# A graph kernel: the permuted graph written over the graph itself, and new shares of the pipeline

## The chip, the cores and the metric

The kernel runs on one core of one Trainium2 chip. The metric is the device time in microseconds of one execution. Engines are named as in the profile: PE (TensorE, matmuls), PEld (its weight loads), DVE (VectorE), ACT (ScalarE), POOL (GpSimd) and SP (SyncE, which issues the transfers).

## The reference

Thirty-two graphs of 512 nodes with 64 features each pass through four layers; after each layer comes x = layernorm(x + layer(x)). Layer 0 averages over neighbours, layer 1 is a Chebyshev filter of order 4, layer 2 a hyperbolic attention over all pairs of nodes, and layer 3 takes quantiles over each node's neighbours. The edited code prepares layer 3:

```python
nb = (adj_ > 0) & (~eye)[None]
m = nb.sum(-1)
rank = jnp.cumsum(nb, axis=-1) - 1
skip = jnp.where(m > T_THRESH, (m + K_DIL - 1) // K_DIL, 1)
removed = nb & do_dil[..., None] & ((rank + 1) % skip[..., None] == 0)
rem = removed | jnp.swapaxes(removed, 1, 2)
adj_d = jnp.where(rem, 0.0, adj_)
# then, for each node and feature: sort the features of its neighbours in adj_d,
# and add up the interpolated quantiles 0.25, 0.5, 0.75 with weights 0.25, 0.5, 0.25
```

## The kernel before

The kernel does not loop over graphs at run time. It records every operation of all 32 graphs (`Order.op`), and a planner (`Order.issue`) then fixes one program order for each engine. An operation belongs to a lane of a graph: front (layers 0 and 1), pairs and tail (layer 2), graph (the code above), gather (fetches the neighbours' features by matmul with one-hot matrices), sort (a sorting network on DVE for nodes in two strips, SB), and head (the strip of the nodes with most neighbours, SH, for two graphs at a time, and the final dense layers). "ends" and "check" run once, near the end.

`STAGES` (line 1415) gives each lane a pair of numbers: the part of the pipeline period, counted from the graph's own number, at which the lane's first and last operations are due. The planner always issues the ready operation with the earliest due time; on PE it stays with the present shape of matmul (64 or 128 columns of weights, 64 or 128 rows) unless another is due much earlier. Where PE would be idle in its plan, it puts in filler matmuls (`stay_active`, lines 1451 to 1454), after leaving a first part of the gap open:

```python
for _ in range(int((t - spare - fill) / 0.11)):   # line 387, fill = 0.3
```

Buffers matter too. A tile is asked for with a tag, and tiles of one tag share a number of buffers. A new tile of a tag is given out only when the last reader of the old one is over. The graph lane has three big tiles of one buffer each, with tags nbT, v and V, each 128 x 4 x 512 in 16-bit floats.

The steps of the graph lane for one graph: nbT marks the neighbours (lines 789 to 791). Matmuls of nbT with a triangular matrix count them in order, ACT and DVE turn the counts into the marks v of the edges to remove (809 to 815). Matmuls of v, its transpose and nbT give the thinned graph V, evicted by ACT with row sums (816 to 827). In `order`, the row sums give each node's position rk by size (834 to 846), and perm is the permutation matrix, made by DVE from it (850 to 852). Matmuls of V with perm give the permuted graph VP, evicted by ACT (853 to 858). Matmuls of VP with the triangular matrix number the neighbours of each node: slot (859 to 864). Matmuls with ones give the counts, from which ACT makes the small one-hot tiles OHM (865 to 875). The gather lane reads slot.

Before the change, perm has nbT's tag and VP has v's. The lane has one PSUM bank, so its matmul groups and their evictions alternate. ACT's program order also holds loads of activation tables, at every change between the logarithm and exponential functions and the sigmoid and tanh functions (lines 391 and 483).

Of the kernel before, what the change touches and what calls it, by code (L numbers as in the profile page):

```python
# [9 lines left out]
F16 = mybir.dt.float16  # L10
# [4 lines left out]
AF = mybir.ActivationFunctionType  # L15
# [5 lines left out]
P = 128  # L21
# [382 lines left out]
def tile_adj_resnorm(ctx: ExitStack, tc: tile.TileContext, x, adj, nodemask, w1k, b1k, att_w, att_b,  # L404
                     w1, b1, w2, b2, out):
    nc = tc.nc
    B, N, D = x.shape
    T = N // P
# [16 lines left out]
    seq = Order(nc, tc)  # L425

    def width(a):
        n = 1
        for d in a.ap[1:]:
            n *= d[1]  # L430
        return n
# [18 lines left out]
    def ts(out, a, s1, s2, op0, op1=None):  # L450
        kw = {} if op1 is None else {"op1": op1}
        vec(lambda: nc.vector.tensor_scalar(out, a, s1, s2, op0=op0, **kw), out, [a], True, (s1, s2))  # L452

    def stt(out, a, s, b, op0, op1):
        vec(lambda: nc.vector.scalar_tensor_tensor(out, a, s, b, op0=op0, op1=op1), out, [a, b], False, (s,))  # L455

    def cp(out, a):
        vec(lambda: nc.vector.tensor_copy(out, a), out, [a], True)
# [18 lines left out]
    def act(out, a, f, bias=None, scale=1.0, accum_out=None, after=None):  # L477
        sc = [x for x in (bias, scale) if isinstance(x, bass.AP)]
        kw = {k: v for k, v in (("bias", bias), ("accum_out", accum_out)) if v is not None}
        n = width(out)  # L480
        table = "exp" if f in (AF.Ln, AF.Exp) else "sig" if f in (AF.Sigmoid, AF.Tanh) else None
        seq.op("ACT", 0.12 + n * 0.83e-3 + 0.09 * len(sc) + (0.2 if accum_out is not None else 0.0),
             0.3, lambda: nc.scalar.activation(out, a, f, scale=scale, **kw), [out, accum_out], [a, after] + sc, table)  # L483
# [7 lines left out]
    def mm(out, w, a, start, stop, pair=False, opens=None):  # L491

        n, m = width(a), width(w)
        if a.dtype == F32:

            t = (1 if pair else 2) * max(0.9e-3 * m, 0.88e-3 * n)
        else:
            t = max(0.058, n * (0.24e-3 if m == D else 0.44e-3))
        def go():
            if opens is not None:  # L500
                seq.open = opens
            return nc.tensor.matmul(out, w, a, start=start, stop=stop)  # L502

        seq.op("PE", t, 0.6, go, [out], [w, a], (64 if w.ap[0][1] <= 64 else 128, 64 if m <= 64 else 128))

    def tr(out, a, ident):
        seq.op("PE", 0.115 if a.dtype == F32 else 0.058, 0.6, lambda: nc.tensor.transpose(out, a, ident), [out], [a, ident],
               (128, 64 if width(a) <= 64 else 128))
# [6 lines left out]
    def bank(dtype=F32, home=None):  # L515
        lane, seq.lane = seq.lane, home or seq.lane
        t = seq.tile(pools["ps"], [P, 512 if dtype == F32 else 1024], dtype, "bank", bufs=BANKS.get(seq.lane, 2))
        seq.lane = lane
        return t
# [21 lines left out]
    UC = const.tile([P, N], F16, name="UC")  # L541
# [3 lines left out]
    onesP = const.tile([P, P], F16, name="onesP")  # L545
# [161 lines left out]
    def col(name):  # L707
        return seq.tile(pools["small"], [P, T], F32, name, 2)
# [121 lines left out]
    def order(b, res):  # L830

        gm = pools["gm"]
        V = res["V"]
        key = col("key")
        stt(key, M3[:, b, :], float(N), iotr, op0=OP.mult, op1=OP.add)
        pt = bank()
        for t in range(T):
            tr(pt[:, t * P:(t + 1) * P], key[:, t:t + 1].to_broadcast([P, P]), identf)
        keyh = col("keyh")
        ts(keyh, key, -0.5, None, op0=OP.add)  # L840
        sg = col("sg")
        for t in range(T):
            junk = seq.tile(gm, [P, N], F16, "junk", 1)
            act(junk, pt, AF.Sign, bias=keyh[:, t:t + 1], scale=-1.0, accum_out=sg[:, t:t + 1])
        rk = col("rk")
        ts(rk, sg, -0.5, 0.5 * N - 1.0, op0=OP.mult, op1=OP.add)

        rkh = seq.tile(pools["keep"], [P, T], F16, "rkh", 8)
        cp(rkh, rk)
        perm = seq.tile(gm, [P, T, N], F16, "perm", 1, "nbT")  # L850
        for t in range(T):
            ts(perm[:, t, :], iotap, rk[:, t:t + 1], None, op0=OP.is_equal)
        VP = seq.tile(gm, [P, T, N], F16, "VP", 1, "v")
        for j in range(T):
            pt = bank()
            for t in range(T):
                mm(pt, V[:, t, j * P:(j + 1) * P], perm[:, t, :], start=(t == 0), stop=(t == T - 1))
            act(VP[:, j, :], pt, AF.Copy)
        slot = seq.tile(pools["keep"], [P, T, N], F16, "slot", 2)
        for j in range(T):  # L860
            pt = bank()
            for k in range(j + 1):
                mm(pt, UC[:, :P] if k == j else UC[:, P:2 * P], VP[:, k, :], start=(k == 0), stop=(k == j))
            act(slot[:, j, :], pt, AF.Copy)
        pt = bank()
        for k in range(T):
            mm(pt, onesP, VP[:, k, :], start=(k == 0), stop=(k == T - 1))
        if b % 2 == 0:
            res["ohm"] = OHM[:, b // 2 % 3]
        dist = seq.tile(gm, [P, H2], F16, "dist")  # L870
        for i in range(P // HM):
            hm, h = slice(i * HM, (i + 1) * HM), i % 2
            act(dist[hm], pt[hm, h * H2:(h + 1) * H2], AF.Abs, bias=npart[hm])
        for i, hm in enumerate((PADS, RANKS)):
            act(res["ohm"][hm, i, b % 2, :], dist[hm], AF.Relu, bias=1.0, scale=-1.0)
        res["slots"] = slot, rkh

    def stage_graph(b, res):
        graph(nmask[:, :, b], res["AT"], M3[:, b, :], res)
        order(b, res)  # L880
# [503 lines left out]
    def within_bounds():  # L1384

        gm, BT = pools["gm"], B * T
        seq.lane = "graph"
        p1, p2, p3 = bank(), bank(), bank()
        ge = [seq.tile(gm, [P, T, N], F16, "ge", 1, t).rearrange("p t n -> p (t n)") for t in ("nbT", "v")]
        ge = [ge[s % 2][:, s // 2 * BT:(s // 2 + 1) * BT] for s in range(K + 1)]  # L1390
        seq.lane = "check"
        m = M3.rearrange("p b t -> p (b t)")

        for s in range(K + 1):
            ts(ge[s], m, float(s), None, op0=OP.is_gt)
        for s in range(K + 1):
            mm(p1[:BT, s:s + 1], ge[s], onesP[:, 0:1], start=True, stop=True)
        cs = seq.tile(gm, [BT, K + 1], F16, "cs")
        act(cs, p1[:BT, :K + 1], AF.Copy)
        mm(p2[:B, :K + 1], graphs[:BT, :], cs, start=True, stop=True)  # L1400
        off = seq.tile(gm, [B, 2, K + 1], F16, "off")
        for i, op in enumerate((OP.is_gt, OP.is_lt)):
            tt(off[:, i, :], p2[:B, :K + 1], limits[:, i, :], op=op)
        bad = seq.tile(gm, [B, 1], F32, "bad")
        reduce(bad, off.rearrange("p i s -> p (i s)"), OP.max)
        badh = seq.tile(gm, [B, 1], F16, "badh")
        cp(badh, bad)
        mm(p3[:1, 0:1], badh, onesP[:B, 0:1], start=True, stop=True)
        ts(flag, p3[:1, 0:1], 0.0, None, op0=OP.is_gt)
# [2 lines left out]

    STAGES = {"front": (-0.6, -0.5), "pairs": (1.2, 1.3), "tail": (0.2, 1.5), "graph": (0.9, 1.0), "gather": (2.7, 2.9),
              "sort": (4.5, 4.6), "head": (4.7, 5.6), "ends": (4.0, 4.5), "check": (3.4, 4.8)}

    nc.scalar.preload_act_table_set("natural_log_exp_and_others")
    with ExitStack() as fast:
# [57 lines left out]
        within_bounds()  # L1477
        seq.issue(80.0, STAGES, stay_active, 0.3)
        seq.lane = "dense"
# [141 lines left out]
    with tc.If(flagv > 0):  # L1621
        with ExitStack() as slow:
# [24 lines left out]
            for h in range(4):  # L1647
                t = cst.tile([P, T, QC * ROWS], BF16, name=f"parts{h}")
# [32 lines left out]
def build(inputs):  # L1681
    import numpy as np
    import concourse.bacc as bacc

    nc = bacc.Bacc("TRN2", target_bir_lowering=False, num_devices=1)
    arrays, args = {}, []
    for name in _INS:
        a = np.ascontiguousarray(inputs[name])
        if a.dtype == np.bool_:
            a = a.view(np.uint8)  # L1690
        arrays[f"in_{name}_dram"] = a
        args.append(nc.dram_tensor(f"in_{name}_dram", a.shape, mybir.dt.from_np(a.dtype), kind="ExternalInput").ap())
    args.append(nc.dram_tensor("out_0_dram", inputs["x"].shape, F32, kind="ExternalOutput").ap())
    with tile.TileContext(nc) as tc:
        tile_adj_resnorm(tc, *args)
    return nc, arrays
# [8 lines left out]
```

## Time and profile before

| | us |
|---|---|
| median of three runs | 2626.49 |
| the three runs | 2620.58, 2626.49, 2630.43 |
| the profiled execution | 2622.02 |
| its span, first to last instruction | 2620.2 |

The span is what the profile divides among the engines; 1.8 us of the profiled execution lie outside it. The shares of busy time, the stretches and the waits that matter are shown in the prediction. Of the groups, these belong to the code that is edited:

```profile
L502 PE MATMUL graph_bank<-graph_perm,graph_V 128*128 128x512 f16 x512 | 141.0, 382 | 16.1 <-DVE graph_perm L452 13.8
L483 ACT ACTIVATE graph_VP<-graph_bank 128x512 f16<-128x512 f32 x128 | 75.5, 590 | 53.7 <-PE graph_bank L502 49.4
```

Each row gives the line, the engine, the tiles (out, then in), the shape and the number of instructions; then the busy time in us and the mean duration of one in ns; then the idle time of the engine just before them and what ended most of it. Nearly all operations are recorded by helpers, so a line is that of a helper (502 is `mm`, 483 is `act`, 448 is `tt`, 452 is `ts`, 455 is `stt`), and the tile's name, which begins with its lane, tells what the row is.

### The profile page before, as it was taken

To read this page: it belongs to the slowest core of one execution; us is meant where nothing else is said; L and a number is where in the kernel's file an instruction comes from. 1 tells how busy PE (TensorE), PEld (TensorE's weight loads), DVE (VectorE), ACT (ScalarE), POOL (GpSimd) and SP (SyncE) were. 2 spreads that over 40 slices of the span, in tenths; PEclk is the share of its full clock that TensorE was granted. 3 is DMA by queue.
4 is the path that set the end of the run, shared out by engine and by line. 5 is a ranking of instruction groups with operands and counts; after the bars stand their busy time and mean duration, and the time that the engine had idled before them with its cause. 6 is when DMAs were issued, how large, how long until landed. Compare 5 with 4: busy or idle time off the path is not lost.

```text
span 2620.2 us, 55667 instructions
## 1 busy us (share of the span) xinstructions
PE 2458.2 (94%) x19641; PEld 1635.4 (62%) x19667; DVE 2402.7 (92%) x9002; ACT 1879.2 (72%) x4406; POOL 815.8 (31%) x1783
## 2 busy tenths in 40 slices
PE   7999999999999999999999999999999999999997
PEld 6666566666666666666656666566666666666655
DVE  3668998999999999999999999999999999998996
ACT  5666677767777777767777677777777778776761
POOL 1233332332343333322333233333323333332210
PEclk9999999999999999999999899999999999998999
DMA  1100000000000000000000000000000000000000
GB/s 38 33 23 21 17 14 15 25 22 23 18 11 22 20 25 21 24 17 13 20 21 25 19 19 13 20 23 22 26 19 13 18 19 26 19 11 3 5 7 8
DMA packets 119723, 49.96 MB, mean 19 GB/s; under 512 B 53740, under 2 KB 119436, under 8 KB 119436
## 3 DMA queue, kind: packets, MB, share of 16 engines
q1 hardware_dynamic: 118272, 46.15, 6.4%
q8 instruction: 156, 2.56, 0.4%
q14 instruction: 131, 1.07, 0.1%
q10 hardware_dynamic: 1164, 0.18, 0.0%
HBM read 37.93 MB, written 8.39 MB: 18 GB/s over the span
## 4 chain that ended last, share of the span: by engine, by line
DVE 72%; PE 18%; ACT 6%; issue 2%; POOL 2%; DMA 0%; ACTq 0%; DVEq 0%
DVE SB L448 17%; DVE SH L448 8%; DVE gather_oh L452 6%; PE front_bank L502 5%; DVE pairs_Q L448 4%; PE gather_bank L502 3%; PE graph_bank L502 3%; DVE pairs_RW L448 3%; PE pairs_bank L502 3%; DVE sort_prod L448 3%; DVE pairs_Wt L455 3%; DVE pairs_L L455 2%; DVE tail_v L448 2%; DVE pairs_EX L448 2%; DVE pairs_RW L455 2%
## 5 line engine op out<-in xcount | busy, mean ns | idle before, releaser
L448 DVE TENSOR_TENSOR SB<-SB 128x448 f32<-128x448 f32 (+11 forms) x1424 | 565.8, 424 | 12.2 <-ACT SB L483 0.7
L502 PE MATMUL gather_bank<-gather_oh,tail_x3h 128*64 128x448 f16 (+5 forms) x5376 | 516.5, 321 | 4.8 <-ACT SB L483 3.4
L502 PEld LDWEIGHTS <-tail_x3h 128*64 128x64 bf16 x5376 | 296.0, 111 | 214.3 <-issue 112.8
L448 DVE TENSOR_TENSOR SH<-SH 128x32 f32<-128x32 f32 (+11 forms) x1744 | 347.4, 246 | 8.1
L502 PE MATMUL pairs_bank<-pairs_FT 67*128 67x512 f32 (+7 forms) x768 | 316.9, 516 | 18.7 <-ACT pairs_EX L483 7.1
L452 DVE TENSOR_SCALAR gather_oh<-graph_slot 128x256 f16<-128x256 f16 (+9 forms) x864 | 252.3, 337 | 25.3 <-PE gather_bank L502 23.5
L502 PE MATMUL front_bank<-front_AT,front_y 128*64 128x512 f32 x768 | 189.5, 607 | 18.5 <-DVE front_y L448 17.0
L502 PEld LDWEIGHTS pairs_bank<-pairs_FT 67*128 67x128 f32 (+1 forms) x768 | 130.2, 194 | 83.2 <-issue 19.7
L502 PE MATMUL graph_bank<-graph_perm,graph_V 128*128 128x512 f16 x512 | 141.0, 382 | 16.1 <-DVE graph_perm L452 13.8
L502 PEld LDWEIGHTS <-graph_nbT 128*128 128x128 f16 x1536 | 113.1, 99 | 57.6 <-issue 17.3
L722 POOL TENSOR_TENSOR front_rs<-front_var,mhalf 128x4 f32<-128x4 f32 x64 | 83.4, 1303 | 201.8 <-DVE front_var L452 152.9
L502 PEld LDWEIGHTS front_bank<-XA,front_AT 128*128 128x128 f32 x1024 | 126.0, 194 | 13.6 <-issue 6.3
L1453 PE MATMUL PA<-zero 128*128 128x256 bf16 x973 | 132.9, 278 | 0.1
L502 PE MATMUL pairs_bank<-FLS,pairs_Wt 128*128 128x66 f32 x1024 | 124.7, 274 | 3.9 <-DVE pairs_Wt L455 3.8
L502 PEld LDWEIGHTS pairs_bank<-FLS,pairs_Wt 128*128 128x128 f32 x1024 | 120.6, 192 | 10.9 <-DVE pairs_Wt L455 7.8
L502 PE MATMUL front_bank<-XA,front_AT 128*128 128x65 f32 x1024 | 124.5, 274 | 0.0
L448 DVE TENSOR_TENSOR pairs_RW<-pairs_RW,pairs_EX 128x640 f32<-128x640 f32 x128 | 104.1, 815 | 18.7 <-ACT pairs_RW L483 18.4
L502 PEld LDWEIGHTS <-tabs 128*128 128x128 f16 x1296 | 78.3, 100 | 64.2 <-issue 54.9
L502 PEld LDWEIGHTS front_bank<-front_AT,front_y 128*64 128x64 f32 x768 | 54.5, 137 | 95.6 <-issue 63.0
L483 ACT ACTIVATE graph_VP<-graph_bank 128x512 f16<-128x512 f32 x128 | 75.5, 590 | 53.7 <-PE graph_bank L502 49.4
L483 ACT ACTIVATE SB<-gather_bank 128x448 f32<-128x448 f32 (+2 forms) x192 | 81.3, 438 | 43.4 <-PE gather_bank L502 43.0
L502 PE MATMUL head_bank<-head_PT,sort_ap 128*64 128x512 f32 x240 | 111.2, 608 | 0.1
(354 smaller groups left out, 6569.8 us busy)
## 6 DMA issues: line engine op xcount, KB each, us to landing
front_A<-in_adj_dram SPq DMA_DIRECT2D x128, 256.0 KB, 2.7
XA<-in_x_dram SPq DMA_DIRECT2D x32, 128.0 KB, 2.2
xs<-tail_x SPq DMA_DIRECT2D x32, 128.0 KB, 1.9
out_dram<-head_zo SPq DMA_DIRECT2D x31, 128.0 KB, 2.0
out_dram<-tail_ends SPq DMA_DIRECT2D x1, 128.0 KB, 2.1
wk<-in_L_gnn_weight_dram ACTq DMA_DIRECT2D x1, 64.0 KB, 3.0
w1s<-in_L_gnn_W_dram ACTq DMA_DIRECT2D x2, 32.0 KB, 2.0
attw<-in_L_gnn_att_W_dram ACTq DMA_DIRECT2D x2, 0.2 KB, 3.2
```

The costliest lines, as they stand in the source:

```text
L448: vec(lambda: nc.vector.tensor_tensor(out, a, b, op=op), out, [a, b])
L452: vec(lambda: nc.vector.tensor_scalar(out, a, s1, s2, op0=op0, **kw), out, [a], True, (s1, s2))
L455: vec(lambda: nc.vector.scalar_tensor_tensor(out, a, s, b, op0=op0, op1=op1), out, [a, b], False, (s,))
L483: 0.3, lambda: nc.scalar.activation(out, a, f, scale=scale, **kw), [out, accum_out], [a, after] + sc, table)
L502: return nc.tensor.matmul(out, w, a, start=start, stop=stop)
L722: seq.op("POOL", 0.8, 0.6, lambda: nc.gpsimd.tensor_tensor(y, v, mhalf, op=OP.pow), [y], [v])
L1453: return nc.tensor.matmul(PA[:, 2 * P:], zero[:, :P], zero, start=False, stop=False)
```

## The change

perm takes the tile of v instead of nbT's. The permuted graph no longer has a tile of its own: its column block j is written over column block j of V, which only the j-th group of matmuls reads. Block j is therefore four runs of 128 columns, and evictions and later matmuls address it so. All nine pairs of `STAGES` are new; in pairs and sort the first bound stays.

```diff
-        perm = seq.tile(gm, [P, T, N], F16, "perm", 1, "nbT")
+        perm = seq.tile(gm, [P, T, N], F16, "perm", 1, "v")
         for t in range(T):
             ts(perm[:, t, :], iotap, rk[:, t:t + 1], None, op0=OP.is_equal)
-        VP = seq.tile(gm, [P, T, N], F16, "VP", 1, "v")
+        def four(a):
+            return a.rearrange("p (t n) -> p t n", n=P)
+        VP = [V[:, :, j * P:(j + 1) * P] for j in range(T)]
         for j in range(T):
             pt = bank()
             for t in range(T):
                 mm(pt, V[:, t, j * P:(j + 1) * P], perm[:, t, :], start=(t == 0), stop=(t == T - 1))
-            act(VP[:, j, :], pt, AF.Copy)
+            act(VP[j], four(pt), AF.Copy)
         slot = seq.tile(pools["keep"], [P, T, N], F16, "slot", 2)
         for j in range(T):
             pt = bank()
             for k in range(j + 1):
-                mm(pt, UC[:, :P] if k == j else UC[:, P:2 * P], VP[:, k, :], start=(k == 0), stop=(k == j))
+                mm(four(pt), UC[:, :P] if k == j else UC[:, P:2 * P], VP[k], start=(k == 0), stop=(k == j))
             act(slot[:, j, :], pt, AF.Copy)
         pt = bank()
         for k in range(T):
-            mm(pt, onesP, VP[:, k, :], start=(k == 0), stop=(k == T - 1))
+            mm(four(pt), onesP, VP[k], start=(k == 0), stop=(k == T - 1))
...
-    STAGES = {"front": (-0.6, -0.5), "pairs": (1.2, 1.3), "tail": (0.2, 1.5), "graph": (0.9, 1.0), "gather": (2.7, 2.9),
-              "sort": (4.5, 4.6), "head": (4.7, 5.6), "ends": (4.0, 4.5), "check": (3.4, 4.8)}
+    STAGES = {"front": (-0.7, -0.2), "pairs": (1.2, 1.4), "tail": (0.7, 1.2), "graph": (1.2, 1.3), "gather": (2.8, 3.3),
+              "sort": (4.5, 5.5), "head": (5.0, 6.2), "ends": (4.3, 4.7), "check": (3.6, 5.6)}
```

## The prediction

> **What bounds the kernel now.** I read the page first: the shares of busy time, then the forty slices.
>
> ```profile
> PE 2458.2 (94%) x19641; PEld 1635.4 (62%) x19667; DVE 2402.7 (92%) x9002; ACT 1879.2 (72%) x4406; POOL 815.8 (31%) x1783
> ...
> PE   7999999999999999999999999999999999999997
> ...
> DVE  3668998999999999999999999999999999998996
> ```
>
> Two engines are nearly full at once. DVE works 2402.7 us of 2620.2, and its empty slices are the first four and the last. PE's 94% contains 1,081 filler matmuls that compute nothing (lines 1453 and 1454), so its real work is smaller. Next I cut the span into ramp, middle and drain:
>
> ```profile
> 0.00:240.00 240.00, 216.77 (x1652) 154.95 (x1652) 143.18 (x522) 152.27 (x336) 61.84 (x211) 0.98 0.10 27
> 240.00:2520.00 2280.00, 2158.65 (x17254) 1422.26 (x17278) 2181.68 (x8167) 1696.86 (x4000) 745.20 (x1564) 0.98 0.07 19
> 2520.00:2620.00 100.00, 82.80 (x739) 58.22 (x738) 77.88 (x316) 30.09 (x71) 8.71 (x8) 0.95 0.04 8
> ```
>
> The columns are PE, PEld, DVE, ACT and POOL busy time. DVE is idle 97 us in the ramp (240 - 143.2), 98 us in the middle and 22 us in the drain: 217 us in all. In the middle PE is idle 121 us. So a change that leaves DVE's work alone can win from these 217 us only, and in the middle PE is right behind DVE. The chain of waits agrees on who leads:
>
> ```profile
> DVE 72%; PE 18%; ACT 6%; issue 2%; POOL 2%; DMA 0%; ACTq 0%; DVEq 0%
> ```
>
> Last, the waits of the middle, DVE's and then PE's:
>
> ```profile
> DVE gather_oh L452 <- PE gather_bank L502: 19.5, 14, 3.0
> DVE pairs_RW L448 <- ACT pairs_RW L483: 12.7, 12, 3.7
> DVE front_st L714 <- PE front_bank L502: 9.7, 23, 2.3
> ...
> PE graph_bank L502 <- DVE graph_perm L452: 12.8, 19, 1.3
> ```
>
> No single wait is large. They are many short misses (1.4 us on average for gather_oh) between engines that are both 95% busy. In the middle no DVE wait of weight belongs to the graph lane, the part that is edited.
>
> [...] a load starts at 88.00, 0.02 us after the activation before it ends, and the next activation starts at 89.30. I take 1.283 us. [...]
>
> **The change part by part.**
>
> *Tiles.* Before, perm takes nbT's tile, so the next graph's nbT must wait for this graph's V-by-perm matmuls. After, perm takes v's tile, and nbT comes free with V's own matmuls. The compiled order shows it. I put a clock on DVE's program order by adding the mean duration of each instruction's row, less 0.072 us of overlap each (the rows add up to 3048.4 us, the busy time is 2402.7, over 9,002 instructions). On this clock nbT of graph 16 stands at 1130 before and 1104 after; perm of graph 16 at 1187 and 1188; nbT of graph 17 at 1200 before, behind perm 16, and at 1178 after, ahead of it. But gather_oh of graph 16 starts at 1225 and 1231: the early start becomes slack inside the lane and reaches nobody downstream. The tile of V is now held until the slot and count matmuls are over; the next V is wanted about 35 us later (one period of 75 us less the 40 us that V is held), so no new wait of weight.
>
> *In place.* The first group's eviction writes the columns of V that only this group read. The order shows no added wait: each next group already waits for that eviction, since the lane has one PSUM bank. I count 0.
>
> *Views.* 448 matmuls read and 128 evictions write four runs of 128 columns in place of 512 in a row. The nearest row is DVE's diagonal operation on nbT, four runs of 128: 414 ns, the same as the contiguous 128x512 f16 comparison with "last" (414 ns). I take 0. The upper end is 448 x 0.022 us (a tenth of the 0.217 us between starts of these matmuls), so 10 us[...].
>
> *Shares.* Instruction counts on DVE, POOL and SP are equal; DVE's work stays 2402.7 us. Three counts move:
> - Fillers: 1,081 become 1,029. In the middle (from the 1,280th to the 14,000th of 15,403 real matmuls) 267 in 63 runs become 189 in 38 runs; ramp and drain together go from 814 to 840. One costs (132.9 + 14.1) / 1081 = 0.136 us. The middle loses 78 x 0.136 = 10.6 us of padding. By line 387 each run also leaves 0.3 us of its gap unfilled: 25 runs fewer x 0.3 = 7.5 us. I take both as gaps that close, 18.1 us. The ends' 26 more fillers (3.5 us) lie where PE waits anyway.
> - Changes between matmuls of 64 and of 128 columns: 946 become 1,022, so 38 pairs more. From the timeline of PE: three transposes (128 columns) start at 1018.16 and take 0.49 us, one alone 0.274, so they are 0.108 apart and the last starts at 1018.38; the gather (64 columns) starts at 1018.58, which is 0.20 later instead of 0.108. Over all such places in the middle without a marked wait, the median excess is 0.098 us one way, 0.192 us the other, and 0.006 where nothing changes. One pair is 0.28 us, 38 pairs 10.6 us. PE has 121 us idle there, so not all is on the path: bounds 18% (PE's share of the chain), 1.9 us, and all of it, 10.6. I take half, 5.3.
> - Table loads: 109 become 121, so 12 x 1.283 = 15.4 us more on ACT, which is 28% idle. Bounds: 6% of it (ACT's share of the chain), 0.9 us, and all, 15.4. I take 1.
>
> *Ramp.* On the DVE clock the first sort begins at 121 instead of 111. On a PE clock built the same way (fillers included) the first gather ends at 209 instead of 203. So 10 us more DVE work is done before the sort starts, which itself starts 6 us later: 4 us of DVE's 97 idle us in the ramp. Bounds: 0, since by graph 3 both orders agree within 1 us on both clocks, and 4. I take 4.
>
> The sum: -18.1 + 5.3 + 1 - 4 = -15.8 us. The profiled execution took 2622.02 us, 1.8 outside its span, which gives 2606.2. It lies 4.5 us under the median of the runs shown (2626.49), from which the sum gives 2610.7. I forecast 2608.
>
> **The rivals.**
> 1. *No change.* The gaps that close in the order don't close on the chip: they were PE waiting for DVE, and DVE's work per graph, 75 us, is the same. For: DVE 72% of the chain; by graph 16 the two orders agree within 6 us on DVE and on PE. Against: DVE has 98 us idle in the middle, some of it waiting for PE. The 18.1 us shrink to a third, 6.0: -6.0 + 5.3 + 1 - 4 = -3.7, so 2618 from the profiled execution and 2623 from the median; I put it at 2620.
> 2. *Slower: ACT's queue.* Each of the 12 added loads stands ahead of evictions on which PE waits, since graph, gather and front have one PSUM bank each; PE stops, and DVE's gather_oh stops behind it (it waits for PE's gather, 19.5 us now). Price: all 15.4 us of the loads and all 10.6 us of the mode changes, with no gap closed and the ramp's 4 us lost: +26.0, so 2648. It decides once more than 18.1 of these 26 us are on the path. For: ACT waited for PE in the graph lane 49.4, 48.1 and 42.5 us, so the pair is tightly coupled there. Against: ACT is 28% idle and 6% of the chain.
> 3. *Larger gain.* From nbT to the counts' first use (skip) graph 16 now has 43 us on the DVE clock instead of 18, and this slack also absorbs the short misses. If a third of DVE's 98 us of middle idle goes, that is -33, so 2592. It counts as faster.
>
> **How the numbers follow.** A measurement of this kernel tells no change within about 0.5%, that is 13 us: 2613.4 to 2639.6. The forecast has 0.37 and the larger gain 0.13, together faster 0.50. No change has 0.27. Slower has 0.23: the ACT mechanism, and short stalls of an order in which every instruction has moved. The forecast's own range is 2596 (views free, both added costs at their lower bounds, 4 us more won) to 2618. For 8 in 10 I reach to 2572, about 20 us under the larger gain, and to 2648, the slower case.
>
> **What would show it.** Right: DVE busy within a few us of 2403; nbT of a graph ahead of perm of the graph before; the middle's DVE idle under 98 us and PE's under 121; 121 table loads at 1.283 us; the view reads at 376 to 383 ns as now. Wrong: a longer row for the graph_V matmuls (the views cost), waits of PE on ACT evictions in the graph and gather banks well above today's 2.5 and 3.4 us (the second rival), or a ramp whose first sort starts later than about 220 us with DVE no fuller.

## The result and the profile after

The median of four executions after the change is 2598.96 us (2592.69 to 2603.44), against 2626.39 for four before. The ratio is 0.9896, with a 95% interval of 0.9865 to 0.9926: faster by 27 us, about 1%. The profiled execution took 2595.93 us (before 2622.02) over a span of 2594.0.

The page of the kernel after, with its shares of busy time, two lines of the slices, and the chain:

```profile
PE 2450.0 (94%) x19596; PEld 1613.0 (62%) x19615; DVE 2400.2 (93%) x9002; ACT 1895.8 (73%) x4418; POOL 789.2 (30%) x1783
...
PE   7999999999999999999999999999999999999997
...
DVE  3668999999999998999999999999999999999996
...
DVE 72%; PE 20%; ACT 4%; issue 2%; POOL 1%; DMA 0%; ACTq 0%; DVEq 0%
```

DVE does the same work (2402.7 us before, 2400.2 now) in a span shorter by 26.2 us. So DVE lost idle time, and the stretches of the kernel after, cut as the prediction cuts the kernel before, tell where (PE, PEld, DVE, ACT, POOL busy, then the granted PE clock):

```profile
0.00:240.00 240.00, 220.56 (x1696) 156.09 (x1698) 142.35 (x516) 157.73 (x340) 62.23 (x209) 0.99 0.10 27
240.00:2494.00 2254.00, 2147.19 (x17197) 1399.26 (x17210) 2180.93 (x8169) 1707.07 (x4009) 718.45 (x1566) 0.99 0.07 19
2494.00:2594.00 100.00, 82.27 (x709) 57.69 (x709) 76.91 (x320) 31.00 (x71) 8.54 (x8) 0.92 0.04 8
```

DVE's idle time is 97.7 us in the ramp (before 96.8), 23.1 in the drain (22.1), and 73.1 in the middle (98.3): the gain is 25 us of DVE's short waits in the middle. The waits of the middle, DVE's (us in total, times, longest):

```profile
DVE front_st L714 <- PE front_bank L502: 16.7, 35, 1.4
DVE gather_oh L452 <- PE gather_bank L502: 9.7, 10, 2.2
...
DVE pairs_RW L448 <- ACT pairs_RW L483: 1.9, 5, 0.9
```

The wait for the gather halves (19.5 to 9.7), that for ACT's pairs_RW almost goes (12.7 to 1.9), and that for the statistics of the front lane grows (9.7 to 16.7). None of the three belongs to the edited lane. The row of the kernel before that reads the permuted graph with contiguous columns:

```profile
L502 PE MATMUL graph_bank<-graph_VP,UC 128*128 128x512 f16 x320 | 91.2, 383 | 2.6 <-ACT graph_VP L483 1.9 <-ACT graph_slot L483 0.5
```

and the rows of the edited code after, with those of all table loads but one (54 and 54 such loads before):

```profile
L502 PE MATMUL graph_bank<-graph_perm,graph_V 128*128 128x512 f16 x512 | 139.3, 380 | 15.0 <-DVE graph_perm L452 10.0 <-ACT pairs_FT L483 2.8 <-DVE tail_s L455 0.9
...
L502 PE MATMUL graph_bank<-graph_V,UC 128*128 128x512 f16 x320 | 90.8, 381 | 1.6 <-ACT graph_V L483 1.3
...
L391 ACT ACT_TABLE_LOAD x60 | 77.0, 1283 | 1.1
L483 ACT ACT_TABLE_LOAD x60 | 77.0, 1283 | 6.0 <-DVE pairs_L L455 5.0
```

Matmuls that read four runs of 128 columns take 381 ns; with contiguous columns they took 383. The reads through views cost nothing that shows here, and ACT's evictions into such runs neither (591 ns in the row of graph_V, 590 before).

**Half the clock.** The granted clock in these rows is a mean over a long stretch. Cut into pieces of 4 us, the trace after shows its grain, here around 1012 us:

```profile
1004.00:1008.00 4.00, 3.51 (x33) 3.04 (x32) 4.00 (x8) 1.77 (x4) 3.67 (x7) 1.00 0.42 124
1008.00:1012.00 4.00, 3.25 (x24) 3.25 (x25) 3.90 (x10) 2.51 (x5) 0.69 (x2) 0.84 0.00 1
1012.00:1016.00 4.00, 4.00 (x21) 4.00 (x21) 3.83 (x14) 2.29 (x8) 0.88 (x5) 0.50 0.00 0
1016.00:1020.00 4.00, 4.00 (x20) 2.70 (x19) 2.67 (x16) 1.16 (x2) 0.71 (x1) 0.50 0.01 2
1020.00:1024.00 4.00, 4.00 (x17) 1.61 (x17) 4.00 (x25) 3.17 (x7) 1.43 (x3) 0.88 0.02 5
```

and the timeline of PE says what came before it (start, duration, and in brackets the idle time with its releaser):

```profile
1005.39 2.12 PE L502 MATMUL pairs_bank<-FLS,pairs_Wt 128*128 128x66 f32 x18
1008.75 0.65 PE L507 MATMUL graph_bank<-identf,graph_key 128*128 128x128 f32 x4 [1.25 <-DVE graph_key L455]
```

PE waits 1.25 us for DVE's graph_key, and from 1010.7 on it runs at half clock for 10 us; DVE, busy 3.90 of 4 us before that, then falls to 2.67 of 4 us (at 1017.84 it has waited 1.33 us for PE's front_bank). The traces have 9 such episodes in the middle after and 11 before, each 3.4, 6.8, 10.2, 13.7 or 17.1 us long. Full-clock time lost in the middle, half the length of the episodes that begin there, since the clock in them is 0.50: 37.5 us before, 25.6 after, in these two executions. The episodes begin on a fixed grid: the first four of the middle after, at 263.20, 348.53, 526.03 and 1010.72, are 25, 52 and 142 times 3.413 us apart. In the piece of this grid just ahead of each of the 20 episodes, PE was idle for 0.65 to 1.86 us. The reverse does not hold: of the 26 pieces at full clock in which PE idled 1.2 us or more, 13 were followed by half clock, and of the 126 with 0.65 us or more, 20. At 2163.50 in the trace after, PE has waited 1.69 us for graph_key, and the clock stays full. So PE's idle time was there each time, but what else decides is open.

Most of the scatter between executions goes with the clock too. Over the 126 executions of the kernel before that were run beside the experiments, on three chips, time and mean granted clock, each taken as the distance from its chip's mean, go together with a correlation of -0.98 and a slope of 17.6 us for each 0.01 of clock. (0.01 of 2617 us is 26 us of full-clock time, so by estimate two thirds of what is lost reaches the end.) In what follows, "at equal clock" means every execution's time moved along this slope to a clock of 0.985. It is a correction by a correlation, with the slope of the kernel before: fit for means between 0.98 and 0.99, an extrapolation for 0.971. Another order can have another slope: the executions of e4 below give 8.8 us for each 0.01 and those of e5 12.7, so a figure at equal clock far from 0.985 is good to some us at best. At equal clock the kernel before stands at 2617.1, 2618.6 and 2619.3 us on the three chips, the kernel after at 2599.4: 18 to 20 us of the 27 are the order of the work, and some 8 us come from the clock that those executions had (before's median implies 0.980; on the other chips it had 0.983 to 0.985). Whether that part belongs to the change is not settled; against the medians of the kernel before on the three chips (2615.5 to 2622.7) the gain would be 17 to 24 us. The traces support the split without the slope: in the middle, DVE is idle 17.8 us inside the half-clock episodes before and 7.4 after, and 80.5 and 65.7 us outside them. Of the 25 us, then, 15 were won at full clock and 10 go with fewer and shorter episodes.

### The profile page after: what moved, and what is told of

Same layout as the page of the kernel before. It is cut to its first block, busy times and chain, and to the rows that moved or that the text cites. A ratio compares the mean times of both kernels' runs of the same rounds, so it can differ in the third digit from the quotient of the medians.

```text
span 2594.0 us, 55595 instructions
## 1 busy us (share of the span) xinstructions
PE 2450.0 (94%) x19596; PEld 1613.0 (62%) x19615; DVE 2400.2 (93%) x9002; ACT 1895.8 (73%) x4418; POOL 789.2 (30%) x1783
## 4 chain that ended last, share of the span: by engine, by line
DVE 72%; PE 20%; ACT 4%; issue 2%; POOL 1%; DMA 0%; ACTq 0%; DVEq 0%
DVE SB L448 17%; DVE SH L448 9%; DVE gather_oh L452 7%; PE front_bank L502 6%; DVE pairs_Q L448 4%; PE gather_bank L502 3%; PE pairs_bank L502 3%; PE graph_bank L502 3%; DVE pairs_RW L448 3%; DVE sort_prod L448 3%; DVE pairs_Wt L455 3%; DVE pairs_L L455 2%; PE head_bank L502 2%; DVE pairs_RW L455 2%; DVE pairs_EX L448 1%
## 5 line engine op out<-in xcount | busy, mean ns | idle before, releaser
L448 DVE TENSOR_TENSOR SB<-SB 128x92 f32<-128x92 f32 (+11 forms) x1424 | 568.8, 425 | 14.4 <-ACT SB L483 1.9
L448 DVE TENSOR_TENSOR SH<-SH 128x32 f32<-128x32 f32 (+10 forms) x1744 | 346.5, 246 | 7.3 <-ACT SH L483 0.9
L502 PE MATMUL pairs_bank<-pairs_FT 67*128 67x512 f32 (+7 forms) x768 | 308.1, 507 | 15.4 <-DVE pairs_EX L455 6.6
L483 ACT ACTIVATE graph_V<-graph_bank 128x512 f16<-128x512 f32 x256 | 151.2, 591 | 84.6 <-PE graph_bank L502 78.8
L502 PE MATMUL front_bank<-front_AT,front_y 128*64 128x512 f32 x768 | 193.1, 618 | 16.7 <-DVE front_y L448 15.6
L502 PEld LDWEIGHTS <-graph_nbT 128*128 128x128 f16 x1536 | 113.5, 99 | 54.5 <-issue 15.5
L502 PE MATMUL pairs_bank<-FLS,pairs_Wt 128*128 128x66 f32 x1024 | 136.5, 274 | 2.5 <-DVE pairs_Wt L455 2.2
L502 PE MATMUL front_bank<-XA,front_AT 128*128 128x65 f32 x1024 | 133.9, 277 | 0.0
L483 ACT ACTIVATE graph_v<-graph_bank,graph_c 128x512 f16<-128x512 f32 x128 | 87.6, 685 | 61.1 <-PE graph_bank L502 50.6
L502 PEld LDWEIGHTS pairs_bank<-FLS,pairs_Wt 128*128 128x128 f32 x1024 | 127.2, 193 | 7.1 <-DVE pairs_Wt L455 5.0
L1457 PE MATMUL PA<-zero 128*128 128x256 bf16 x925 | 122.6, 279 | 0.2
L502 PEld LDWEIGHTS front_bank<-fold,front_sums 128*128 128x128 f32 x768 | 97.0, 191 | 25.5 <-issue 5.2
```

The lines of the kernel that those rows point to most:

```text
L448: vec(lambda: nc.vector.tensor_tensor(out, a, b, op=op), out, [a, b])
L1457: return nc.tensor.matmul(PA[:, 2 * P:], zero[:, :P], zero, start=False, stop=False)
```

## The experiments

Each kernel was compared with the kernel before on the same chip. "Loss in the middle" is the full-clock time lost to the half-clock episodes that begin in the middle (240 us to 100 us before the end) of its profiled execution. "Mean clock" is that of its executions.

| kernel | ratio to before, 95% interval | mean clock | at equal clock, to before (us) | loss in the middle (us) |
|---|---|---|---|---|
| e1 tiles alone | 1.0022 (1.0004 to 1.0041) | 0.983 | +7.9 | 29.0 |
| e2 shares alone | 0.9934 (0.9909 to 0.9959) | 0.984 | -13.8 | 30.7 |
| e3 perm in nbT's tile | 0.9930 (0.9907 to 0.9953) | 0.985 | -12.0 | 39.2 |
| e4 two shares moved by 0.05 | 1.0042 (1.0028 to 1.0056) | 0.991 | +24.0 | 16.9 |
| e5 no fillers in the middle | 0.9952 (0.9937 to 0.9967) | 0.979 | -23.0 | 45.8 |
| e6 182 more fillers | 0.9904 (0.9873 to 0.9934) | 0.991 | -15.5 | 17.1 |
| e7 60 more table loads | 0.9962 (0.9947 to 0.9978) | 0.987 | -4.2 | 23.9 |
| e8 182 more pairs of mode changes | 0.9923 (0.9893 to 0.9953) | 0.993 | -7.1 | 11.9 |
| e9 new tiles, shares searched | 0.9944 (0.9925 to 0.9962) | 0.982 | -19.3 | 37.3 |
| e10 old tiles, shares searched | 1.0002 (0.9974 to 1.0030) | 0.971 | -22.8 | 64.6 |
| e11 e9 with 181 more fillers | 0.9931 (0.9902 to 0.9960) | 0.985 | -16.6 | 32.4 |
| e12 before with 179 more fillers | 0.9988 (0.9969 to 1.0007) | 0.987 | +1.2 | 37.3 |

The column at equal clock has 95% intervals of 0.6 to 1.7 us from the scatter of the executions, the doubt about the slope not counted; the changed kernel stands at -18 to -20 in it. The ratios are measured and don't depend on the correction.

### Which half of the change (e1, e2, e3)

e1 keeps the new tiles and takes back the shares:

```diff
-    STAGES = {"front": (-0.7, -0.2), "pairs": (1.2, 1.4), "tail": (0.7, 1.2), "graph": (1.2, 1.3), "gather": (2.8, 3.3),
-              "sort": (4.5, 5.5), "head": (5.0, 6.2), "ends": (4.3, 4.7), "check": (3.6, 5.6)}
+    STAGES = {"front": (-0.6, -0.5), "pairs": (1.2, 1.3), "tail": (0.2, 1.5), "graph": (0.9, 1.0), "gather": (2.7, 2.9),
+              "sort": (4.5, 4.6), "head": (4.7, 5.6), "ends": (4.0, 4.5), "check": (3.4, 4.8)}
```

> The tiles of the change with the shares of the kernel before. Theory A (the freed tile alone gives the gain: nbT can go early, the middle gets denser): 2598 to 2610 us, DVE idle in the middle near the changed kernel's 73 us. Theory B (the shares give it): about 2626 us. Theory C (only the pair of tiles and shares fits, since shares chosen for one set of buffers are wrong for another): 2635 us or more. The order has 381 fillers in the middle against 267 before and 189 in the changed kernel, which speaks for C: 114 fillers more at 0.136 us are 15 us, so 2640 us.

e2 is the other half: the kernel before with the new shares only. Shown against the changed kernel, with the lines that follow from the second one cut:

```diff
-        perm = seq.tile(gm, [P, T, N], F16, "perm", 1, "v")
+        perm = seq.tile(gm, [P, T, N], F16, "perm", 1, "nbT")
...
-        VP = [V[:, :, j * P:(j + 1) * P] for j in range(T)]
+        VP = seq.tile(gm, [P, T, N], F16, "VP", 1, "v")
```

> The shares of the change with the tiles of the kernel before. Theory A (tiles): about 2626 us. Theory B (shares): about 2599 us. Theory C (both are needed): in between or above 2626. The order has 247 fillers in the middle (267 before, 189 in the changed kernel): 58 more than the changed kernel, 8 us, so I expect 2610 us.

e3 is the changed kernel with perm back in nbT's tile. The permuted graph still overwrites V, so v comes free early and nbT late.

```diff
-        perm = seq.tile(gm, [P, T, N], F16, "perm", 1, "v")
+        perm = seq.tile(gm, [P, T, N], F16, "perm", 1, "nbT")
```

> The changed kernel, but perm takes nbT's tile as before; the permuted graph is still written over V. This frees v early and not nbT. If the gain of the tiles is nbT's early start, this equals the shares alone (2610 us, within 0.5% of that run), and its view reads cost nothing: 380 ns a matmul. If freeing v is what helps, it equals the changed kernel, 2599 us.

The stretch of the middle in e1, then in e2:

```profile
240.00:2525.40 2285.40, 2159.43 (x17436) 1435.83 (x17455) 2179.78 (x8171) 1710.78 (x4014) 723.68 (x1565) 0.99 0.07 19
```

```profile
240.00:2501.90 2261.90, 2150.06 (x17200) 1405.22 (x17224) 2180.91 (x8146) 1710.11 (x4003) 712.82 (x1562) 0.99 0.07 19
```

DVE's idle time in the middle is 105.6 us with the tiles alone and 81.0 with the shares alone, against 98.3 before and 73.1 with both. So the shares carry most of the gain: alone they win 0.66% of the change's 1.04%. The 2610 us expected of e2 were near (2605), the 2640 us expected of e1 were not (2626): the added fillers did not cost their length. At equal clock the tiles are worth +8 us with the old shares and, from the table, a gain of 4 to 6 us more with the new ones. By the ratios alone this second figure isn't safe, since the intervals of e2 and of the change overlap; at equal clock it is larger than the difference between the chips. e3 has e2's time within its interval and loses the advantage again: what the tiles give goes with nbT's tile coming free early, while in-place writing and views show no gain, and a cost of at most about 2 us (e3 less e2 at equal clock). That the early start itself wins these 4 to 6 us is not shown: the tiles also change the whole planned order, and e4 shows that such a change alone can move the time by more.

### How firm is a choice of shares (e4)

```diff
-    STAGES = {"front": (-0.7, -0.2), "pairs": (1.2, 1.4), "tail": (0.7, 1.2), "graph": (1.2, 1.3), "gather": (2.8, 3.3),
+    STAGES = {"front": (-0.7, -0.2), "pairs": (1.2, 1.4), "tail": (0.65, 1.25), "graph": (1.2, 1.3), "gather": (2.75, 3.25),
```

> The changed kernel with two lanes' shares moved by 0.05: tail from 0.65 to 1.25 and gather from 2.75 to 3.25. Theory D (the planner's order is so sensitive that a small move of the shares changes the time by as much as the whole gain): 2625 us or more; the order has 482 fillers in the middle against 189, 40 us, so up to 2639. If the shares act smoothly: 2599 us within 0.3%.

Two shares moved by 0.05 cost 1.5% and undo the change. DVE's wait for the gather in e4, in the list of waits of the middle:

```profile
DVE gather_oh L452 <- PE gather_bank L502: 27.9, 18, 4.1
```

It was 9.7 us over 10 times. The expectation of a sensitive order, 2625 us or more, came true (2631). The planner's order isn't a smooth function of the shares, so no reason such as "graph is due later" can be read off them.

### Fillers and the clock (e5, e6, e12)

e5 drops the 189 fillers of the middle and nothing else (`real` counts the real matmuls; its first value is cut):

```diff
-                for _ in range(int((t - spare - fill) / 0.11)):
+                real += 1
+                for _ in range(0 if 1280 < real <= 14000 else int((t - spare - fill) / 0.11)):
```

> The changed kernel without the 189 fillers in the middle of PE's order (ramp and drain keep theirs). If the fillers themselves lie on the path (they run in front of work that is ready), the time falls by up to 189 x 0.136 = 26 us, to 2573. If PE waits for other engines there anyway, it stays at 2599 us within 0.3% and the fillers only mark gaps; PE's busy time falls by 26 us and its idle time grows by as much.

e6 adds 182 fillers in the middle, spread evenly, each between two matmuls of 128 columns (cut: the first values of the counters, and the argument that gives a filler its number of weight columns):

```diff
+                real += 1
+                if 1280 < real <= 14000 and real - due >= 66 and seen == ops[i][7] == (128, 128):
+                    before[e], due = self.pin(filler(128), before.get(e)), real
+                seen = ops[i][7]
```

> The changed kernel with 182 more fillers of 128 weight columns in the middle of PE's order, spread evenly, each between two matmuls of 128 columns: 182 x 0.136 = 25 us more PE work. If PE's 107 us of idle time in the middle absorb it: 2599 us, up to 2604. If PE is on the path half the time: 2611. If all of it counts: 2624.

e12 does to the kernel before what e6 does to the kernel after.

> The kernel before with 179 more fillers spread over the middle in the same way. If part of the change's gain is the higher granted clock (0.986 against 0.982), the kernel before gains 0.3% or more from fillers alone, 2613 us; if the gain is the order alone, it stays within 0.2% or slows by up to 24 us.

The middle of e5, then of e6:

```profile
240.00:2505.30 2265.30, 2146.21 (x17026) 1392.22 (x17023) 2182.85 (x8169) 1708.26 (x4010) 721.19 (x1566) 0.98 0.07 19
```

```profile
240.00:2489.50 2249.50, 2152.19 (x17377) 1405.83 (x17375) 2179.58 (x8163) 1707.35 (x4009) 718.77 (x1565) 0.99 0.07 19
```

e5's time rose, which neither of its expectations had. e6's ratio is that of the change, as if PE's idle time took the fillers in. Taking 25.7 us of fillers away (189 x 0.136) leaves PE's busy time where it was (2147.2 to 2146.2), and adding 24.8 us raises it by 5.0. The clock accounts for most of the rest in e5 (20.2 us more lost) and for less than half of it in e6 (8.5 us less lost); what makes up the remaining 11 us of e6 is open. The slices of e5's page show the lower clock where the page after has only nines (a digit is the mean over 65 us):

```profile
PEclk9999989999999998999999999999999999999999
```

The middle of e5 has 15 half-clock episodes, the kernel after 9, e6 has 7. In this order fewer fillers go with more half-clock time: the mean clock goes from 0.979 (e5) over 0.985 (after) to 0.991 (e6). At equal clock a filler costs 0.02 us of its 0.136: (2599.4 - 2595.6) / 189 from e5 to after, (2603.1 - 2599.4) / 182 from after to e6. With the slope of e5's own executions it would be 0.004 from e5 to e6, so 0.02 is an upper estimate. The clock gives back more than that from e5 to the kernel after (ratio 0.9952 against 0.9896), and e6 is 13.7 us faster than e5 in the mean of their executions, on the same chip. From the kernel after to e6 the clock rises again, but the ratio shows no further gain (0.9904). e12 shows only a trace of it: 0.003 of clock, and a ratio that is no different from 1.

### The two added costs (e7, e8)

e7 loads a table twice at each of the 60 changes to the exponential set, 60 loads or 77 us more on ACT:

```diff
+                before[e] = self.pin(self.nc.scalar.preload_act_table_set("natural_log"), before.get(e))
```

> The changed kernel with a second table load ahead of each of its 60 loads of the logarithm and exponential set: 60 x 1.283 = 77 us more on ACT, five times what the change added. The second rival (loads are on the path) expects 2676 us, the forecast's price (6%) 2604. ACT's 28% of idle time decides.

e8 is e6 with fillers of 64 columns, so that each makes a pair of mode changes (PE goes from matmuls of 128 columns of weights to 64 and back):

```diff
-                    before[e], due = self.pin(filler(128), before.get(e)), real
+                    before[e], due = self.pin(filler(64), before.get(e)), real
```

> As the run with 182 more fillers, at the same places and of the same 256 columns, but with 64 weight columns instead of 128: each now costs a pair of mode changes, 364 changes in all. The difference to that run is the price of 182 pairs: 182 x 0.28 = 51 us if all is on the path, 25 us at the half that the forecast took, 9 us at 18%.

Sixty loads cost 15 us at equal clock (-4.2 against -19), a fifth of their length: more than the forecast's 6%, far less than all. The change's 12 loads are then 3.0 us, if they stand in places like these. The middle of e8:

```profile
240.00:2497.60 2257.60, 2187.63 (x17389) 1415.47 (x17386) 2182.18 (x8166) 1711.51 (x4009) 722.15 (x1566) 0.99 0.07 19
```

PE is busy 35.4 us more than in e6, 0.195 us for each of the 182 pairs, but the time rises by only 8.4 us at equal clock, 0.046 us a pair. The change's 38 pairs are 1.8 us.

### Could better shares be found (e9, e10, e11)

By then the first orders ranked in time as they rank in the number of fillers in the middle, and I held that the planner's own reckoning could find better shares. Some 2,400 settings were planned; e9 takes those with the earliest planned end for the new tiles, e10 for the old.

```diff
+    STAGES = {"front": (-0.7, -0.2), "pairs": (1.25, 1.3), "tail": (1.1, 1.15), "graph": (1.2, 1.3), "gather": (2.9, 3.25),
+              "sort": (4.6, 5.5), "head": (5.0, 6.2), "ends": (5.05, 6.25), "check": (3.35, 4.2)}
```

> The changed tiles with other shares, picked from about 2,400 settings as those whose planned order ends first. Its order has 89 fillers in the middle (changed kernel 189, before 267) and 1,146 mode changes. In the five orders measured so far the time rises with the fillers in the middle: 189, 247, 247, 267, 381, 482 stand at ratios 0.990, 0.993, 0.993, 1.000, 1.002, 1.004. If these gaps are what the shares and tiles work through, this one is the fastest: 2585 us, ratio 0.985. If they are not (or if fillers are needed for the clock), 2600 us or more.

```diff
+    STAGES = {"front": (-0.75, -0.3), "pairs": (1.2, 1.25), "tail": (0.35, 1.4), "graph": (0.9, 0.95), "gather": (2.7, 2.9),
+              "sort": (4.6, 4.7), "head": (4.6, 5.65), "ends": (2.7, 4.2), "check": (3.55, 5.45)}
```

> The tiles of the kernel before, with shares picked in the same way from as many settings: 225 fillers in the middle. If nbT's early start is needed for the gain, this stays at or above the shares alone (ratio 0.993, 2603 us). If good shares reach as far without the tile, it equals the changed kernel (0.990).

e11 is e9 with e6's fillers.

> The changed tiles with the searched shares, and the 181 evenly spread fillers of 128 columns besides. Taking the fillers away from the middle cost 0.5%, and 182 more cost nothing and raised the granted clock from 0.986 to 0.991. So with only 89 left this order should gain from more: 0.3% below the searched shares without them, 2577 us; if the clock is already full, equal to them within 0.2%.

e9 missed the 2585 us expected, and the theory that few fillers in the middle make a fast order fell with it (89 in e9, 225 in e10, 189 after). e10's time fits the expectation that nbT's early start is needed, but not for that reason. At equal clock the search had worked: e9 equals the changed kernel, and e10 is 22.8 us under the kernel before, with the old tiles. But e10's clock of 0.971 takes back 23.8 us (0.0135 below the kernel before on its chip, at 17.6 us for each 0.01). The clock's slices of e10, and two stretches of 65 us:

```profile
PEclk9999989899999999999999989999999999999999
```

```profile
325.00:390.00 65.00, 61.85 (x473) 42.02 (x472) 54.59 (x232) 42.00 (x100) 17.16 (x39) 0.89 0.06 16
650.00:715.00 65.00, 62.42 (x531) 42.33 (x526) 64.52 (x252) 50.24 (x117) 18.73 (x41) 1.00 0.04 11
```

At a clock of 0.89 DVE works 54.6 us of 65, at 1.00 it works 64.5, while PE is 95 and 96% busy. Why this order has 20 half-clock episodes in the middle, against 9 after the change, is open; that its figure at equal clock is extrapolated has to be kept in mind; and fillers in e10 were not tried. A count without the slope gives it less: outside the episodes and the 6.8 us after each, DVE's idle time in the middle is 76.7 us before, 59.4 after and 63.4 in e10, which is 13 us under before. Either way good shares without the new tiles come near, so the tiles' 4 to 6 us hold for one set of shares. In e11 the fillers cost 2.7 us at equal clock and raise the clock by 0.002: not told apart from e9, which was one of its two expectations. No version was clearly faster than the changed kernel: e6's median is lower (2591.37), but its ratio of 0.9904 is the same.

## Why the prediction was right, and where its sum was not

The forecast was 2608 us, with a sum of -15.8; measured were -26.1 between the profiled executions and about -19 at equal clock. The change is faster and inside the forecast's range, but that the sum came near was luck: the terms are not what the runs show. Its largest part, 18.1 us for gaps that close, is not what was won, and shorter waits of DVE that it didn't price took its place.

| term of the sum | forecast | by the runs |
|---|---|---|
| 78 fillers fewer in the middle | -10.6 | at most -1.6 at equal clock (78 x 0.02) |
| 25 filler runs fewer, 0.3 us left open in each | -7.5 | not seen by itself |
| 38 pairs of mode changes | +5.3 | +1.8 (e8) |
| 12 table loads | +1 | +3.0 (e7) |
| the ramp | -4 | 0: DVE idle 96.8 before, 97.7 after |
| views and in-place writing | 0 | 0 (row of 381 ns; at most about 2, e3) |

- *Gaps that close.* The step "I take both as gaps that close, 18.1 us" is the one that stood on a wrong reading. It took fillers for time on the path. Fillers cost 15% of their length or less at equal clock, and in this order the mean clock rose with their number (0.979 in e5, 0.985 after, 0.991 in e6). So dropping 78 of them by itself would, by estimate from these three, rather lose time than win it. By subtraction, -19 less (-1.6 + 1.8 + 3.0) leaves -22 us at equal clock for a better order. This is a remainder and not a measurement; what the traces show are shorter waits of DVE, and why this order shortens them is open. The prediction had the size of these waits right (98 us in the middle) but priced their fall by the filler count, which e9 and e10 showed to be no measure.
- *The tiles.* nbT of the next graph does start ahead of perm (1164.36 against 1172.30 in the timeline after; 1196.32 after 1181.73 before). "The early start becomes slack inside the lane and reaches nobody downstream" is not borne out: the tiles move the time at equal clock by +8 us with the old shares and by -4 to -6 with the new. By which way they do so was not followed.
- *Table loads and mode changes.* The taken values were off by 2.0 and 3.5 us, in opposite directions; the loads lay between their bounds (0.9 to 15.4), the pairs at their lower one of 1.9. The mode change's length from the trace (0.28 us a pair) was near the 0.195 of PE time that e8 shows; how much of it reaches the end was overrated.
- *The ramp.* The first sort starts at 224.06 instead of 214.11. DVE has then done 126.55 us of work instead of 118.04, 8.5 us more, but the sort starts 10 us later and not 6, so no idle time is won (in the first 240 us DVE works 142.35 us, before 143.18). That was named as the sign that this step is wrong, and it is.
- *The range.* Its lower end, 2596, doesn't follow from the terms given for it: the two costs at their bounds and 4 us more won make -23.3, which is 2598.7 from the profiled execution and 2600.5 from the forecast. The measured 2598.96 lies at that edge.
- *The rivals.* No change is excluded by the interval. The queue of ACT is not what happened: PE waits less for ACT's evictions into SB and of the graph (2.7 and 1.3 us, as the list of PE's waits after shows, beside 3.4 and 2.5 before). PE's waits for ACT in the whole graph lane stay (5.5, before 5.1), since the one for pairs_FT is new, and those in all lanes fall from 19.8 to 14.9. And 60 extra loads cost 15 us, so 12 at such places can't cost 15.

```profile
PE graph_bank L502 <- ACT pairs_FT L483: 2.8, 3, 1.1
PE gather_bank L502 <- ACT SB L483: 2.7, 5, 0.9
...
PE graph_bank L502 <- ACT graph_V L483: 1.3, 2, 0.8
```

- The larger gain (-33) had the mechanism that the runs favour: waits of DVE in the middle, all over the lanes, fall by 25 us, 10 of them inside half-clock episodes, which no rival had. The measured median is nearer to its 2592 us than to 2608. Its cause, the slack in the graph lane alone, is too narrow: in e2 nbT's tile comes free no earlier than before, and e2 wins more than half.

## What to carry to other kernels

Before padding is counted as time won, look at what it does to the clock: a filler of 0.136 us cost 0.02 us or less here, and where PE idled 1.2 us or more within 3.413 us at full clock, 3.4 to 17 us at half clock followed 13 times in 26. Compare executions at equal granted clock where a per cent matters, and look at pieces of a few microseconds, since a mean of 0.98 hides stretches at 0.50. A buffer that comes free earlier lost 8 us with one set of shares here and won 4 to 6 with another, so a planner's order must be measured each time: one picked for its early planned end (e10) ran no faster than before, at a clock of 0.971, and shares moved by 0.05 cost 1.5%.

## What was not expected of the hardware

- The half clock after pieces of 3.413 us in which PE had idled as little as 0.65 us (20 times in 126; 13 in 26 where it had idled 1.2 us or more), for 3.4, 6.8, 10.2, 13.7 or 17.1 us, and that the mean clock goes with nearly all of the scatter between executions of one program (correlation -0.98, 2609 to 2647 us for the kernel before).
- PE's busy time stayed the same (2146 us) with 26 us of its instructions taken away, mostly because the remaining ones ran longer at half clock (20 us more of full-clock time lost). Here busy time was no measure of work.
- A pair of changes between 64 and 128 columns adds 0.195 us to PE's busy time and only 0.046 us to the kernel's at equal clock (e8 less e6).
